# A selective scan on one core: TensorE's scan-stage work put into two row groups of 64

## The chip, the core and the metric

The kernel runs on one core of a Trainium2 chip. A core has TensorE (matrix multiplies and transposes, into PSUM), VectorE, ScalarE, GpSimd (called POOL in the profile) and SyncE (SP, which here issues nearly all DMAs). They run side by side and wait for each other through semaphores. The metric is the device time of one execution in microseconds, as the median of several runs. All data are fp32.

## The reference

Two residual blocks work on x of shape (8, 56, 56, 192). Block 0 is a gated Toeplitz mixer (group norm, three projections, Toeplitz products along both image axes, an output projection). Block 1 is a visual state-space block, and nearly all of the time goes there:

```python
xz = gn(x) @ W_in.T                     # 192 -> 2 x 384;  xc, z = split
xc = silu(depthwise_conv3x3(xc))        # (8, 384, 56, 56)
xs = [four snake orders of the image, and the four reversed]    # K = 8 directions, L = 3136
dts, B, C = split(einsum(xs, x_proj_weight), [12, 16, 16])      # per direction
delta = softplus(einsum(dts, dt_projs_weight) + bias)           # (8, K, 384, L)
h[l] = exp(delta[l] * A) * h[l-1] + (delta[l] * xs[l]) * B[l]   # 16 states a channel
y[l] = sum over states of h[l] * C[l];  y += D * xs             # summed over directions
out = x + (layernorm(y) * silu(z)) @ W_out.T
```

## The kernel before

For each of the 8 images the kernel runs three stages one after the other: a preparation (input projection, 3x3 convolution, the three stored snake orders written to DRAM as xo), the **scan stage**, and a last stage that reads the directions' outputs back, sums them and does the layer norm, the gate and the output projection. Block 0 runs ahead of all this. The change touches the scan stage alone, and the weights that the host lays out for it.

**Chunks, groups, pairs, units.** A direction's 3136 positions are cut into chunks of W = 127. Four chunks make a group (508 positions); a direction has six such groups and a last one of a single chunk. The 384 channels are NB = 3 blocks of 128, d = 0, 1, 2. A pair is two chunks of one block, and it has four units: chunk c = 0, 1, each with states 0 to 7 (half 0) and 8 to 15 (half 1). So a full group is 24 units, a direction 150, an image 1200, the kernel 9600. One unit is:

- `products` (L733), TensorE: the scan's additive term bx, 8 states x 127 positions, from dut (the transposed delta*x, positions on partitions) and bd (the B values laid on a diagonal). It is made in two turns; in each, positions 0 to 63 and 64 to 126 are two row groups of TensorE that write to different banks, and the banks are swapped in the second turn. A ScalarE instruction (`between`) stands between the turns.
- `exps` (L688), ScalarE: da = exp(delta*A), four instructions a unit on average, a pair of das ahead at most. `before` (L756), ScalarE: copies the carried state into column 0 of bx. `keep` (L774), ScalarE: takes the carry out after a pair.
- `scan` (L761), VectorE: one scan instruction over 8 x 128 elements.
- `times_c` (L779), POOL: hc = h * C.
- `sums` (L789), TensorE: eight transposes of hc[:, n] (128 channels x 127 positions), accumulated in PSUM, so they sum over the states: yps, positions on partitions. It takes four tiles of 127 x 128 (pair parity, chunk) in one bank.
- `summed` (L699), ScalarE: yps to yt after a pair, and a store to DRAM after three.

**What a group needs ahead of its units.** Weights (once per direction) and xs are loaded (`load`). `project` (L540), TensorE: px, the 12 + 16 + 16 projected rows, padded to XR = 64, one matmul of 508 columns for each d, accumulated. `projected` (L553), ScalarE: pxs = px + a bias row of 1. `to_dram` and `broadcast` (SP) send the C rows through DRAM to all partitions (cbt); `diagonal_out` (L631) and `diagonal_in` (L637) do the like for B with bd. `steps` (L575), TensorE: pd = dt_w x pxs, 13 rows, for each d; `stepped` (L584), ScalarE, copies it to delta; `softplus` (L588), ScalarE, once for all three blocks, with a load of another activation table on either side of it. `product` (L612), POOL: du = delta * xs for a chunk, 128 x 381. `turn` (L617), TensorE: three transposes of du into pt; `turned` (L621), ScalarE: copies pt to dut. px, pd and pt share one PSUM buffer in a bank of its own (pool pmisc, one buffer). A last group of one chunk has `all_steps` (L595) and `all_stepped` (L604), one step for all three blocks.

**What sets the order.** The kernel writes each engine's order out by hand, step by step: in step t the loop issues the second bx turn of unit t + 1, the first of t + 2, `keep` of t - 1, `summed` of t - 4, `sums` of t - 3, planned ScalarE work, up to two exponentials, `before` of t + 1, the `between` instruction, planned VectorE work, the scan of t, planned TensorE work, `times_c` of t - 1, planned POOL and SP work, more exponentials as a credit allows, and "late" work (softplus). `plan` says at which step, counted from the first unit f of the group, planned work comes. bx has three buffers, h and hc four each. Engines are kept apart by PSUM tensor and bank: an access waits for the earlier ones of other engines in the program's order that touch the same bank of the same tensor.

## Time and profile before

| | us |
|---|---|
| Median of 3 runs (32,992.14 to 33,007.02) | 32,998.84 |
| The profiled execution's own time | 33,035.09 |
| Its span, first to last instruction | 33,033.3 |
| Its eight scan stages together | 25,014.3 |
| All the rest | 8,019.0 |

The mean granted TensorE clock is 0.968 over the span and 1.00 in the scan stages. A row of the profile names the line, the engine, the operation, what is written from what, partitions x elements, and how often; then busy time and mean duration in ns, or start and length in us. "PEld" is TensorE's weight load, which runs beside its matmuls. The part after "<-" in brackets is how long the engine was idle before and what ended that; "issue" means that nothing seen in the profile did. A matmul in fp32 appears as two instructions, a transpose as one.

### The profile page before, as it was taken

Reading aid. Unit: us, or ns where it says so; the run is one execution under the profiler, and the core shown is the slowest. Engines: PE = TensorE matmul, PEld = TensorE weight load, DVE = VectorE, ACT = ScalarE, POOL = GpSimd, SP = SyncE. Lnnn points to the kernel's source line nnn. Section 1 sums busy time; section 2 is a strip of 40 time slices with the busy share of each in tenths; the row PEclk is TensorE's granted clock in tenths of the full one; section 3 lists DMA queues with packets and bytes.
Section 4 is the critical chain, followed back from the end, with each engine's and each line's share of the span. In section 5 each row is a group of like instructions: output and inputs, shape, how many; then the busy total and the mean of one; then the engine's idle time right before and its main releaser. Section 6 shows DMA issues by size and latency. Waiting matters only on the chain. (4 is left out here: it accounts for less than half of the span.)

```text
span 33033.3 us, 535851 instructions
## 1 busy us (share of the span) xinstructions
PE 30106.0 (91%) x195376; PEld 20579.6 (62%) x195376; DVE 23832.6 (72%) x13236; ACT 23299.1 (71%) x63562; POOL 22361.9 (68%) x11632
## 2 busy tenths in 40 slices
PE   8999899979998899979998899979998899979998
PEld 5555566646665566646665566646665566646665
DVE  3444588848886588848886688848886688848886
ACT  2332588838886588838886688838885688838885
POOL 0000588838886588838886588838885688838885
PEclk9999999989999999989999999989999999989999
DMA  3222344444444444444444344444444344444444
GB/s 78 60 60 56 116 126 127 127 127 125 126 129 132 120 127 128 126 126 128 125 126 138 119 125 126 129 128 124 127 128 133 118 129 125 126 127 130 125 126 132
DMA packets 4719499, 3974.35 MB, mean 120 GB/s; under 512 B 3678496, under 2 KB 4401888, under 8 KB 4611008
## 3 DMA queue, kind: packets, MB, share of 16 engines
q1 hardware_dynamic: 4558272, 3778.58, 40.3%
q10 hardware_dynamic: 158592, 161.47, 1.9%
q8 instruction: 1552, 25.43, 0.3%
q14 instruction: 1083, 8.87, 0.1%
HBM read 3406.62 MB, written 547.17 MB: 120 GB/s over the span
## 5 line engine op out<-in xcount | busy, mean ns | idle before, releaser
L761 DVE TENSOR_TENSOR_SCAN h<-da,bx 128x1024 f32<-128x1024 f32 x9600 | 21447.9, 2275 | 3899.2 <-ACT bx L756 2956.6
L779 POOL TENSOR_TENSOR hc<-h,cbt 128x1016 f32<-128x1016 f32 x9600 | 20694.4, 2177 | 2470.8 <-DVE h L761 1973.9
L688 ACT ACTIVATE da<-delta,A_logs 128x254 f32<-128x254 f32 x39936 | 17115.8, 490 | 856.1 <-PE bx L733 807.1
L733 PE MATMUL bx<-bd,dut 63*128 63x252 f32 (+1 forms) x76800 | 11032.5, 404 | 1071.2 <-ACT bx L756 376.8
L789 PEld LDWEIGHTS yps<-ident,hc 128*127 128x127 f32 x76800 | 9246.5, 190 | 3384.3 <-issue 2081.0
L789 PE MATMUL yps<-ident,hc 128*127 128x128 f32 x76800 | 11065.2, 287 | 196.4 <-ACT bx L756 142.7
L733 PEld LDWEIGHTS bx<-bd,dut 63*128 63x128 f32 (+1 forms) x76800 | 6506.3, 187 | 4540.3 <-ACT da L688 878.0
L422 POOL MEMSET xp<- 128x58 f32 x96 | 10.3, 194 | 5692.5 <-DMA x<-x1d 3395.9
L612 POOL TENSOR_TENSOR du<-delta,xs 128x381 f32<-128x381 f32 x1600 | 1605.7, 1004 | 712.7 <-ACT bx L756 477.3
L1004 ACT ACTIVATE sq<-yc 128x1344 f32<-128x1344 f32 x56 | 74.0, 1322 | 2111.9 <-DMA yk<-yt 1781.2
L540 PE MATMUL px<-xs,xpw 128*64 128x508 f32 (+1 forms) x2688 | 1304.4, 576 | 226.7 <-DMA xs<-xo 198.4
L575 PE MATMUL pd<-pxs,dtw 13*128 13x508 f32 x2304 | 1296.6, 642 | 17.9 <-ACT delta L584 10.7
L584 ACT COPY delta<-pd 128x508 f32<-128x508 f32 x1152 | 669.7, 581 | 727.2 <-PE pd L575 721.4
L756 ACT COPY bx<-h 128x8 f32<-128x8 f32 x4608 | 753.2, 163 | 594.1 <-PE bx L733 324.2
L446 PE MATMUL pc<-xp,dg 128*128 128x448 f32 x3024 | 1138.0, 538 | 0.0
L774 ACT COPY carry<-h 128x8 f32<-128x8 f32 x4608 | 884.1, 192 | 320.9 <-DVE h L761 302.6
L756 ACT COPY bx<-carry 128x8 f32<-128x8 f32 x4992 | 820.4, 164 | 400.3 <-PE bx L733 369.1
L468 POOL COPY xo<-xc 128x672 f32<-128x672 f32 x112 | 80.6, 749 | 1392.8 <-issue 754.8
L699 ACT COPY yt<-yps 127x256 f32<-127x256 f32 (+1 forms) x2496 | 890.2, 357 | 175.6 <-PE yps L789 122.3
L446 PEld LDWEIGHTS pc<-xp,dg 128*128 128x128 f32 x3024 | 571.2, 189 | 565.5 <-issue 565.5
L470 DVE COPY xo<-xc 128x672 f32<-128x672 f32 x112 | 90.3, 848 | 1129.3 <-ACT xc L453 1129.3
L406 DVE TENSOR_SCALAR x1n<-x,gstat 96x448 f32<-96x448 f32 x224 | 103.6, 505 | 1078.8 <-DMA x<-x1d 803.5
(121 smaller groups left out, 17121.0 us busy)
## 6 DMA issues: line engine op xcount, KB each, us to landing
cbt<-cd SPq DMA_DIRECT2D x768, 2032.0 KB
bd<-bd SPq DMA_DIRECT2D x1600, 512.0 KB
xs<-xo SPq DMA_DIRECT2D x384, 762.0 KB
yt<-yt SPq DMA_DIRECT2D x1536, 190.5 KB
yk<-yt ACTq DMA_DIRECT2D x1792, 84.0 KB
yk<-yt SPq DMA_DIRECT2D x1792, 84.0 KB
xo<-xo SPq DMA_DIRECT2D x168, 672.0 KB
xc<-xc SPq DMA_DIRECT2D x112, 672.0 KB
```

The costliest lines, as they stand in the source:

```text
L446: nc.tensor.matmul(pc, dg[:, d, j, :], xp[d][:, t * RT + dy : t * RT + dy + RT, dx : dx + HW], start=(j == 0), stop=(j == 8),)
L540: nc.tensor.matmul(self.px[:, : self.n], weights[self.k][0][:, d], self.xs[:, d], start=(d == 0), stop=(d == NB - 1),)
L575: nc.tensor.matmul(self.pd[:, : self.n], weights[self.k][1][:, d * 128 : (d + 1) * 128], self.pxs[0 : R + 1], start=True, stop=True,)
L612: nc.gpsimd.tensor_mul(self.du, self.delta[:, :, part], xs[:, :, part])
L688: yield nc.scalar.activation(da[:, : G.ncs, n, 1:], src.rearrange("p (c t) -> p c t", t=W), AF.Exp, scale=an[:, G.k, self.d, col : col + 1],)
L699: nc.scalar.copy(G.yt[:, : G.ncs, self.d * 128 : (self.d + 1) * 128], yps[:, self.i % 2, : G.ncs])
L733: mm = nc.tensor.matmul(self.bx[:, 4 * q : 4 * q + 4, 1 + 64 * r : 1 + 64 * r + nr], dut[rows, P.d * 128 : (P.d + 1) * 128], bd[rows, n0 : ...
L756: return nc.scalar.copy(self.bx[:, :, 0], prev)
L761: nc.vector.tensor_tensor_scan(self.h.rearrange("p n t -> p (n t)"), das[2 * (P.i % 2) + self.half][:, self.c].rearrange("p n t -> p (n t) ...
L774: nc.scalar.copy(P.carry[:, P.d, states(self.half)], self.h[:, :, W])
L779: nc.gpsimd.tensor_tensor(self.hc, self.h[:, :, 1:], G.cb[P.s][:, states(self.half), self.c * W : (self.c + 1) * W], ALU.mult,)
L789: nc.tensor.matmul(yps[:, self.P.i % 2, self.c], lhsT=self.hc[:, n], rhs=ident, start=(self.half == 0 and self.c == 0 and n == 0), stop=(s ...
```

## The change

- The two PSUM pools of one bank become one tensor `acc` of two banks, [128, 2, 512]. Its first half-banks hold yps, its second half-banks a scratch `mis` for px, pd and the turns. Index r of the bank is the row group (partitions 0 to 63 and 64 to 127 of the operands).
- `sums`: each transpose becomes two, of the channels of each row group, with a moving operand of 64 columns instead of 128; 16 loads and 16 matmuls a unit instead of 8 and 8.
- `project`: the contraction over 128 channels is split in two row groups that write partial sums to two banks, in two calls e of 254 positions each; XR grows to 128, so that the 12 step rows stand at partitions 0 and again at 64. `projected` copies bank 0 with the bias, and the new `added`, VectorE, adds bank 1.
- `steps`: the first 254 positions by row group 0, the last 254 by row group 1, with the weights given twice and padded with zeros to 64 rows. `stepped` copies both banks in one instruction. `all_steps` and `all_stepped` split in the like way.
- `turn`: three transposes become six halves. `turned` copies both banks in one instruction.
- `product`: odd chunks go to VectorE, even ones stay on POOL.
- The plan: TensorE's planned work comes at even steps and the read of it by ScalarE one step later. `projected` at f - 23 and f - 21 (one at f - 19 before), `stepped` at f - 19, - 17, - 15 (f - 17, - 15, - 13), softplus at f - 13 (f - 12), `to_dram` and the first `diagonal_out` at f - 20 (f - 19), loads at f - 36 (f - 34). The turns stay at f - 10, - 8, - 6, - 4.
- In the loop, planned ScalarE work is issued ahead of `sums` instead of after it, and planned VectorE work after the scan instead of ahead of it.

The diff, cut to its core:

```diff
-            pmisc = st.enter_context(tc.tile_pool(name="pmisc", bufs=1, space=PSUM))
-            pyp = st.enter_context(tc.tile_pool(name="pyp", bufs=1, space=PSUM))
+            pacc = st.enter_context(tc.tile_pool(name="pacc", bufs=1, space=PSUM))
...
-            yps = pyp.tile([W, 2, 2, 128], F32, name="yps")
+            acc = pacc.tile([128, 2, 512], F32, name="acc")
+            yps = acc[:, :, :256].rearrange("p r (i c x) -> p r i c x", i=2, c=2)
+            mis = acc[:, :, 256:]
+            def rows(r):
+                return slice(64 * r, 64 * r + 64)
...
+                def project(self, e):
+                    h = self.half
+                    e = self.n // h - 1 - e if self.rev else e
+                    for d in range(NB):
+                        for r in range(2):
+                            nc.tensor.matmul(
+                                mis[:, r, :h],
+                                weights[self.k][0][rows(r), d],
+                                self.xs[rows(r), d, e * h : e * h + h],
+                                start=(d == 0),
+                                stop=(d == NB - 1),
+                            )
...
+                    self.part = self.pxs[:, e * h : e * h + h]
+                    self.src = src[:, 1]
+                    nc.scalar.activation(self.part, src[:, 0], AF.Identity, bias=pxb)
+                def added(self):
+                    nc.vector.tensor_add(self.part, self.part, self.src)
...
-                    nc.tensor.matmul(
-                        self.pd[:, : self.n],
-                        weights[self.k][1][:, d * 128 : (d + 1) * 128],
-                        self.pxs[0 : R + 1],
...
+                    for r in range(2):
+                        nc.tensor.matmul(
+                            mis[:, r, :h],
+                            weights[self.k][1][rows(r), d * 128 : (d + 1) * 128],
+                            self.pxs[rows(r), r * h : r * h + h],
...
-                    nc.gpsimd.tensor_mul(self.du, self.delta[:, :, part], xs[:, :, part])
+                    eng = nc.vector if c % 2 else nc.gpsimd
+                    eng.tensor_mul(self.du, self.delta[:, :, part], xs[:, :, part])
...
-                        nc.tensor.transpose(self.pt[:, d * 128 : (d + 1) * 128], self.du[:, d], ident)
+                        for r in range(2):
+                            nc.tensor.transpose(
+                                mis[:W, r, 64 * d : 64 * d + 64], self.du[rows(r), d], ident[rows(r), rows(r)]
+                            )
...
                     for n in range(HN):
-                        nc.tensor.matmul(
-                            yps[:, self.P.i % 2, self.c],
-                            lhsT=self.hc[:, n],
-                            rhs=ident,
-                            start=(self.half == 0 and self.c == 0 and n == 0),
...
+                        for r in range(2):
+                            nc.tensor.matmul(
+                                yps[:W, r, self.P.i % 2, self.c],
+                                lhsT=self.hc[rows(r), n],
+                                rhs=ident[rows(r), rows(r)],
+                                start=(self.half == 0 and n == 0),
...
+                credit -= 0.5 * do("ACT", t)
                 if (U := unit(t - 3)) is not None:
                     U.sums()
-                credit -= 0.5 * do("ACT", t)
...
-                do("DVE", t)
                 if (U := unit(t)) is not None:
                     U.scan()
+                do("DVE", t)
                 do("PE", t)
```

## The prediction

> **What bounds the kernel now.** I read the busy times first, then the eight scan stages one by one, then one group of 24 units in order of time. (A difference of 0.2% is about what a measurement of this kernel can tell from none.)

> The page's busy times, over the whole span:

> ```profile
> PE 30106.0 (91%) x195376; PEld 20579.6 (62%) x195376; DVE 23832.6 (72%) x13236; ACT 23299.1 (71%) x63562; POOL 22361.9 (68%) x11632
> ```

> The same by stretches: first the sum over the eight scan stages, then one regular group of the fourth (busy us of each engine, then clock and DMA):

> ```profile
> sum 25014.30, PE 23821.09 PEld 16885.12 DVE 21447.60 ACT 21667.94 POOL 22127.35; mean PE 2977.64 PEld 2110.64 DVE 2680.95 ACT 2708.49 POOL 2765.92
> ```

> ```profile
> 15799.87:15861.12 61.25, 59.31 (x410) 42.22 (x409) 53.63 (x24) 53.57 (x150) 55.44 (x30) 1.00 0.44 125
> ```

> So 25,014 us of the 33,033 are scan. There a group takes 61.25 us and TensorE is busy for 59.31 of it, against 53.6 for VectorE and ScalarE: TensorE bounds. What does it spend it on? Its timeline in that group (start, length, engine, line):

> ```profile
> 15801.32 1.15 PE L789 MATMUL yps<-ident,hc 128*127 128x128 f32 x8
> 15802.40 1.13 PE L733 MATMUL bx<-bd,dut 64*128 64x256 f32 x8
> 15803.45 1.15 PE L789 MATMUL yps<-ident,hc 128*127 128x128 f32 x8
> ...
> 15806.67 1.07 PE L540 MATMUL px<-xs,xpw 128*64 128x508 f32 x2
> 15807.67 1.13 PE L733 MATMUL bx<-bd,dut 64*128 64x256 f32 x8
> ```

> A unit costs 1.08 (sums) + 1.05 (bx) = 2.14 us from start to start; px adds 1.00. Now the weight loads of another stretch:

> ```profile
> 8509.46 0.73 PEld L733 LDWEIGHTS bx<-bd,dut 64*128 64x128 f32 x8
> 8510.52 0.96 PEld L789 LDWEIGHTS yps<-ident,hc 128*127 128x127 f32 x8 [0.33 <-issue]
> ```

> Before the sums (128 rows) the weight path stands 0.33 us waiting for nothing but issue, in unit after unit, because bx ran in row groups of 64. Net work is less: eight loads take 0.96 and three (L617) 0.41, so 0.11 per transpose, 0.88 for eight; bx x8 takes 1.13 and the x4 of a lone turn 0.70, so 0.43 for two passes in both row groups, 0.86 for four. 0.88 + 0.86 = 1.74: 0.40 us of 2.14 is changing the array's shape.

> [...]two half loads must overlap. [...]the loads of bx show it, two of 0.18 us within 0.19 us, four within 0.30:

> ```profile
> 8509.46 0.19 PEld L733 LDWEIGHTS bx<-bd,dut 64*128 64x128 f32 x2
> ...
> 8509.46 0.30 PEld L733 LDWEIGHTS bx<-bd,dut 64*128 64x128 f32 x4
> ```

> [...]In the group above the sums already waited 0.7 us for the yt copy of their bank.

> **The change, part by part, for a group of 24 units.**
> - *Sums*: 16 loads and 16 matmuls of 64 moving columns for 8 and 8 of 128. In parallel row groups the pair costs one load, 0.11: still 0.88 a unit. That 64-row transposes run is seen at L263 (eight of 64 columns in 0.63 us, 0.056 each), and that TensorE takes an instruction every 26 ns at L276 (22 loads in 1.22 us, a matmul to each); four per 0.11 us are needed. No drain on either side: 24 x 0.40 = 9.6 us gone.
> - *px*: three steps of 1.00 become two bursts of 3 x 2 passes x 254 columns in both groups: 0.215 us per pass (bx, 256 columns), 1.28 each, 2.56 in all for 3.0.
> - *pd*: 3 x 1.05 (15818.22 to 19.26) becomes 3 x 2 x 0.213 = 1.28. *Turns*: 12 loads of 0.11, 1.32.
> - TensorE's sum: 24 x 1.74 + 2.56 + 1.28 + 1.32 = 46.9, where the same sum of before is 24 x 2.14 + 3.0 + 3.15 + 1.4 = 58.9. It stops being the bound; the next is VectorE.
> - *VectorE*: back-to-back scans start 2.19 us apart (x2 in 4.46, each 2.27), 52.6 for 24. New: two `added` of 254 columns from PSUM, by L1002 (448 columns 616 ns, 1.05 ns a column from L1024 and L1028) 0.41 each; two du of 381 columns, by L1024 0.55 each. 1.9 us, all on the path: the scan behind them waits. 54.5.
> - *POOL* loses two du of 1.00: 24 x 2.17 + 2.0 = 54, not quite the bound. *ScalarE* has two pxs copies of 254 columns (0.47 by the 679 ns for 508 and 362 for 127) for one of 0.68, +0.26 on 53.6 that overlap at their ends.
> - *New waits*: yps and the scratch share two banks, so in the nine steps with a read of the scratch (2 pxs, 3 delta, 4 dut) the sums stand behind ScalarE's copy, which stands behind carry (end of a scan) and yt: by carry 0.2, yt 0.37, copy 0.58 it ends about 1.1 us after the scan, while TensorE wants the bank at 0.6 (it waits for the same scan to free a bx buffer, then makes half a bx, 0.43). 9 x 0.5 = 4.5 us of TensorE at most, behind which bx wait; TensorE has 54.5 - 46.9 = 7.6 to spare, and bx are made a unit ahead. I take nothing, at most 0.2 each on the path (1.8). After a pxs, both `added` and the next sums wait for each other's bank; 0.1 each.
> - *DMAs*: weights grow from 13 to 128 rows and 64 to 128 columns, once per direction and 24 units ahead; to_dram goes a step earlier and now waits for `added` on SP, with the diagonal writes queued behind it; the reads that need them come over ten steps later. Nothing, with steps of 2.3 us as the cover; without it bd would come late.
> - *What is late next*: the two stalls that ScalarE makes. A pd step today:

> ```profile
> 15818.22 1.11 PE L575 MATMUL pd<-pxs,dtw 13*128 13x508 f32 x2
> ...
> 15819.42 0.58 ACT L584 COPY delta<-pd 128x508 f32<-128x508 f32 x1 [0.73 <-PE pd L575]
> ...
> 15820.71 0.17 ACT L756 COPY bx<-carry 128x8 f32<-128x8 f32 x1
> ...
> 15820.98 2.29 DVE L761 TENSOR_TENSOR_SCAN h<-da,bx 128x1024 f32<-128x1024 f32 x1 [0.83 <-ACT bx L756]
> ```

>   The 0.73 us wait for a late pd makes the scan 0.83 late. With pd done 0.6 + 0.88 + 0.43 = 1.9 us after the step began, before ScalarE asks in the next, this goes (three pd, and 0.85 + 1.52 at the px). The second stays:

> ```profile
> 15834.55 1.28 ACT L588 ACT_TABLE_LOAD   x1
> 15835.84 1.47 ACT L588 ACTIVATE delta<-delta 128x1524 f32<-128x1524 f32 x1
> 15837.22 0.16 ACT L756 COPY bx<-h 128x8 f32<-128x8 f32 x1
> ...
> 15837.48 4.57 DVE L761 TENSOR_TENSOR_SCAN h<-da,bx 128x1024 f32<-128x1024 f32 x2 [1.45 <-ACT bx L756]
> ```

>   Softplus holds ScalarE for 2.75 us and the scan for 1.45. It moves a step, and I keep 1.5. Steps with carry, yt, copy, two exponentials and the bx copy hold about 1.95 us of ScalarE in 2.19; I add 0.8 for these and for the bank turns.

> The sum: 52.6 + 1.9 + 1.5 + 0.8 = **56.8 us** a group, 4.45 or 7.3% less. I give every scan stage that share: 0.0727 x 25,014 = 1,817. The other 8,019 us are not touched. 33,035 (the profiled execution's own time, 2 us over its span) - 1,817 = 31,218; the median of the runs lies 36 lower: **31,180**.

> **Rivals.**
> - *The half loads of the transposes do not overlap.* No row of before shows transposes in two row groups at once. Bound from below: 0.11 a pair. From above: 0.22, a unit of 16 x 0.11 + 0.86 = 2.62, a group of 24 x 2.62 + 5.2 = 68.1 + 1.9 of idle as now = 70: +14.3%, 36,600 us, **slower**. It decides from 0.17 a pair ((61.25 - 1.9 - 5.2) / 24 = 2.26, less 0.86, by 8). Against it: the bx loads. I take 0.11. Chance 0.08.
> - *Bank turns tie TensorE to ScalarE.* If each of the nine delays the scan by 0.5, 4.5 us go and the gain with them: 33,000. Against: the unit of lead. At 0.3 each 2.7 are lost, 32,300. Chance 0.12 for both together, of which 0.06 within or above 0.2% of before.
> - *VectorE becomes nearly the whole bound*, softplus hidden by a ScalarE that TensorE no longer holds up (its waits for bx, pd and px are 1.6 + 1.1 + 2.2 + 0.8 = 5.7 us a group): 54.5 + 0.5 = 55.0, -10.2%, 30,450. Chance 0.15.
> - *It does not do what it says*: a drain stays between sums and bx, say 0.2 of the 0.4. TensorE 46.9 + 4.8 = 51.7, still under 54.5; bx come later, about 58.5: 31,900. Inside the likeliest case's range.

> **Numbers.** The likeliest case, 0.65, has 30,600 to 31,950 for its own range. To it come the larger gain, and half of the bank turns: 30,450 to 32,500 holds about 0.83; left out are the serial loads and turns that eat everything. Faster by over 0.2%: 0.65 + 0.15 + 0.06 = 0.86; within: 0.05; slower: 0.09.

> **What would show it.** In the profile after, sums of x16 in about 0.9 to 1.0 us, no 0.33 idle before them, TensorE near 47 to 50 us in a group of 57, scans 2.19 apart in most steps, no scan late at a delta copy, one late by 1 to 1.5 at softplus, and VectorE's busy share in the scan near 95%. Sums of 1.7 us or TensorE still at 97% would prove the sum wrong; so would scans late after every turn, with TensorE waiting for dut, delta or pxs.

## The result, and the profile after

The changed kernel takes 38,623 us (38,534 to 38,680) where the kernel before, beside it on the chip, took 33,002: a ratio of 1.1701 [1.1679, 1.1724]. The forecast was 31,180 us and faster: it is **wrong in sign**.

The page of the kernel after, busy times and granted clock over the span (40 slices, in tenths of full speed; before, nearly every digit was 9):

```profile
PE 34813.8 (90%) x286960; PEld 30031.1 (78%) x286960; DVE 24584.5 (64%) x14836; ACT 23597.0 (61%) x64010; POOL 21923.7 (57%) x10864
...
PEclk9998777676777677677767767677767676776776
```

TensorE was to be busy for less time, and is busy 4,708 us more. The busy times of the eight scan stages, summed, and then of one regular group (busy us of PE, PEld, DVE, ACT and POOL; last the clock, the DMA share and GB/s):

```profile
sum 30605.90, PE 28506.27 PEld 26280.30 DVE 22183.77 ACT 21961.62 POOL 21703.39; mean PE 3563.28 PEld 3285.04 DVE 2772.97 ACT 2745.20 POOL 2712.92
```

```profile
18074.62:18149.89 75.27, 72.57 (x639) 68.31 (x638) 55.45 (x29) 54.36 (x150) 54.33 (x28) 0.68 0.39 113
```

The scan stages grew by 5,592 us (25,014 to 30,606), the span by 5,585: all of it lies there. A regular group takes 75 us for 61, and TensorE's clock in it is 0.68 for 1.00. So the first question is not what TensorE does but how fast its clock runs. The same group again, cut where its clock changes (columns as above):

```profile
18084.30:18107.70 23.40, 22.58 (x276) 19.36 (x274) 22.23 (x12) 20.61 (x62) 18.98 (x9) 1.00 0.12 20
18107.70:18111.60 3.90, 2.02 (x28) 1.76 (x26) 2.60 (x2) 3.85 (x8) 3.89 (x4) 0.94 0.74 78
18111.60:18145.00 33.40, 33.40 (x242) 32.62 (x244) 23.30 (x12) 22.18 (x61) 22.79 (x12) 0.50 0.66 207
```

In the first stretch the clock is full and VectorE is busy for 22.2 of 23.4 us: this is the kernel that was forecast. In the second TensorE is busy for only 2.0 of 3.9 us. In the third it runs at half clock, and is busy for **all** of 33.4 us: slowed by two, it bounds the group. The trace's clock record has the fall at 18111.14 and the return 47.8 us later.

The timeline of the first stretch (start, length, engine, line), a run of scans with one pd step and two units in it:

```profile
18090.60 19.70 DVE L796 TENSOR_TENSOR_SCAN h<-da,bx 128x1024 f32<-128x1024 f32 x9
...
18101.37 0.65 PE L594 MATMUL acc<-pxs,dtw 64*128 64x254 f32 x4
...
18102.07 0.58 ACT L603 COPY delta<-acc 128x508 f32<-128x508 f32 x1
...
18104.76 1.07 PEld L825 LDWEIGHTS acc<-ident,hc 64*127 64x127 f32 x16
...
18104.97 1.00 PE L825 MATMUL acc<-ident,hc 64*127 64x64 f32 x16
...
18105.80 1.08 PE L768 MATMUL bx<-bd,dut 63*128 63x252 f32 x8
...
18106.71 1.01 PE L825 MATMUL acc<-ident,hc 64*127 64x64 f32 x16
```

Sixteen half transposes take 1.00 us, nothing idles before their weight loads in this unit, a unit is 1.74 us from sums to sums (18104.97 to 18106.71), the copy of delta waits for nothing, and nine scans run without a gap. Then softplus, at the second stretch:

```profile
18108.58 1.28 ACT L609 ACT_TABLE_LOAD   x1
18108.78 1.00 PE L825 MATMUL acc<-ident,hc 64*127 64x64 f32 x16
...
18109.87 1.47 ACT L609 ACTIVATE delta<-delta 128x1524 f32<-128x1524 f32 x1
...
18111.56 2.07 PE L768 MATMUL bx<-bd,dut 64*128 64x256 f32 x8 [1.78 <-ACT bx L791]
18111.60 4.56 DVE L796 TENSOR_TENSOR_SCAN h<-da,bx 128x1024 f32<-128x1024 f32 x2 [1.30 <-ACT bx L791]
...
18113.40 1.82 PE L825 MATMUL acc<-ident,hc 64*127 64x64 f32 x16
```

The scan is 1.30 us late, where 1.5 was forecast. But TensorE, which is ahead now, stands 1.78 us idle (1.04 at this place before), and from the fall at 18111.14 on the same bx x8 takes 2.07 us for 1.08 and the same sums 1.82 for 1.00. A unit then costs TensorE about 3.4 us (scans at 18074.62 and 18077.98, both in the half-clock stretch before this one) against VectorE's 2.19.

### The profile page after: what moved, and what is told of

Read it like the earlier page. It is cut to its first block, busy times and chain, and to the rows that moved or that the text cites. A ratio compares the mean times of both kernels' runs of the same rounds, so it can differ in the third digit from the quotient of the medians.

```text
span 38618.7 us, 724883 instructions
## 1 busy us (share of the span) xinstructions
PE 34813.8 (90%) x286960; PEld 30031.1 (78%) x286960; DVE 24584.5 (64%) x14836; ACT 23597.0 (61%) x64010; POOL 21923.7 (57%) x10864
## 5 line engine op out<-in xcount | busy, mean ns | idle before, releaser
L768 PE MATMUL bx<-bd,dut 64*128 64x256 f32 (+1 forms) x76800 | 15567.8, 521 | 1742.0 <-ACT bx L791 516.9
L825 PEld LDWEIGHTS acc<-ident,hc 64*127 64x127 f32 x153600 | 14920.2, 256 | 1422.3 <-issue 769.9
L825 PE MATMUL acc<-ident,hc 64*127 64x64 f32 x153600 | 14072.4, 333 | 425.7 <-ACT delta L603 130.3
L768 PEld LDWEIGHTS bx<-bd,dut 64*128 64x128 f32 (+1 forms) x76800 | 10366.8, 258 | 2949.9 <-ACT da L722 922.0
L422 POOL MEMSET xp<- 128x58 f32 x96 | 10.2, 190 | 5674.3 <-DMA x<-x1d 3404.6
L551 PE MATMUL acc<-xs,xpw 64*128 64x254 f32 x9984 | 1853.6, 505 | 247.0 <-DMA xs<-xo 208.4
L551 PEld LDWEIGHTS acc<-xs,xpw 64*128 64x128 f32 x9984 | 1450.0, 265 | 299.1 <-issue 243.4
L734 ACT COPY yt<-acc 127x256 f32<-127x256 f32 (+1 forms) x2496 | 900.2, 361 | 1144.5 <-PE acc L643 426.3
L643 PE MATMUL acc<-ident,du 64*127 64x64 f32 x9600 | 1371.3, 391 | 53.7 <-POOL du L638 39.3
L643 PEld LDWEIGHTS acc<-ident,du 64*127 64x127 f32 x9600 | 1233.6, 307 | 63.7 <-POOL du L638 45.0
L649 ACT COPY dut<-acc 127x384 f32<-127x384 f32 x1600 | 763.5, 477 | 541.0 <-PE acc L643 541.0
```

Of the source, the lines that this page charges most:

```text
L551: nc.tensor.matmul(mis[:, r, :h], weights[self.k][0][rows(r), d], self.xs[rows(r), d, e * h : e * h + h], start=(d == 0), stop=(d == NB - 1),)
L643: nc.tensor.transpose(mis[:W, r, 64 * d : 64 * d + 64], self.du[rows(r), d], ident[rows(r), rows(r)])
L649: nc.scalar.copy(dut.rearrange("w (d r x) -> w r d x", d=NB, r=2), mis[:W, :, : 64 * NB].rearrange("w r (d x) -> w r d x", d=NB),)
L734: nc.scalar.copy(out.rearrange("w c (r x) -> w r c x", r=2), yps[:W, :, self.i % 2, : G.ncs])
L768: mm = nc.tensor.matmul(self.bx[:, 4 * q : 4 * q + 4, 1 + 64 * r : 1 + 64 * r + nr], dut[at, P.d * 128 : (P.d + 1) * 128], bd[at, n0 : n0 ...
L825: nc.tensor.matmul(yps[:W, r, self.P.i % 2, self.c], lhsT=self.hc[rows(r), n], rhs=ident[rows(r), rows(r)], start=(self.half == 0 and n == 0),
```

## The experiments

**Theory.** Two factors: a *fall* where ScalarE holds TensorE for some half of a window, and a *length*, set by what runs at half clock: the half-row sums do not bring the clock back, the dense px burst does. (In the trace of the kernel after, 495 phases of half clock begin in a scan stage; px ran in the last window of 3.41 us of 426 of them, and in 364 of the 4,848 windows in which the clock stayed low.) **Rivals**: the bank turns or late data are the loss and the low clock only follows from the idle time; or the clock is low because TensorE has slack, whatever its instructions are. Below, "falls" are the phases of half clock in each trace's clock record that lie in a scan stage (in every run eight of them, one a stage, had begun just before it), and "half-clock time" is their time there; the table after the last run has them all.

**1. Filler bursts.** Three bursts a group of six matmuls like px, into the scratch, read by nobody.

```diff
+            for G in groups:
+                for step in (-14, -12, -2):
+                    if G.nch > 1 and ("PE", G.first + step) not in plan:
+                        at("PE", G.first + step, G.warm)
```

> The changed kernel with three bursts of TensorE work added to each full group, at the even steps f - 14, f - 12 and f - 2 that have none: six matmuls of 254 columns (twelve passes, 1.28 us at full clock) into the scratch, which nobody reads; nothing else differs. Clock theory (TensorE's granted clock falls to one half at the softplus stall and the light mix of bx and half transposes cannot lift it again): the bursts keep it up or lift it within a few steps, mean clock in the scan stage over 0.9 where it is 0.70 now, a group 57 to 60 us for 75, 31,000 to 32,500 us in all. Rival (the turns on the shared banks, or the number of instructions, cost the time and the low clock only follows from the waiting): 3 x 1.28 us more work for TensorE in a group, 38,600 to 41,000 us, the clock still near 0.7.

Measured: 36,208 us, 1.0960 [1.0943, 1.0976], clock 0.87. Added work, 2,400 us less time: against the rival, but short of the range of the theory, which had the bursts keep the clock up as well. A phase of half clock lasts 15.6 us for 35.9; the falls stay (478 for 503).

**2. Exp for Softplus**, to be rid of the table loads around it (1.28 us each in the kernel before); log(1 + x) is left out.

```diff
-                    nc.scalar.activation(v, v, AF.Softplus)
+                    nc.scalar.activation(v, v, AF.Exp)
```

> The changed kernel with Exp in the place of both Softplus activations (the logarithm of 1 + x is left out), so that ScalarE loads no other table around them: the stall of 2.75 us becomes 1.5. Clock theory: TensorE is not idle long enough in regular groups for the clock to fall there, so the mean clock of the scan stage rises from 0.70 to 0.85 or more (low phases are left where directions begin), 32,000 to 34,500 us. Rival (bank turns): the 2 x 1.28 us of table loads saved in a group are all there is to win, at most 64 x 6.2 x 2.6 = 1,000 us, 37,600 us or more, clock as now.

Measured: 35,860 us, 1.0858 [1.0842, 1.0874]. Slower than the theory's range and far faster than the rival's: the stall sets off much of the loss, but not all. 440 falls are left, at other waits.

**3. The sums in 128 rows again**, eight transposes into one bank; all else of the change stays.

```diff
-                        for r in range(2):
-                            nc.tensor.matmul(
-                                yps[:W, r, self.P.i % 2, self.c],
-                                lhsT=self.hc[rows(r), n],
-                                rhs=ident[rows(r), rows(r)],
+                        nc.tensor.matmul(
+                            yps[:W, self.c],
+                            lhsT=self.hc[:, n],
+                            rhs=ident,
```

> The changed kernel with its sums put back to full transposes of 128 rows and 128 moving columns, into one half of bank 0 (no second buffer for the other pair; the wait for yt is there already). px, pd, turns, du, bank turns and the order stay as changed. Clock theory, in the form that the half-width moving operand of the sums is what makes the mix too light: the clock comes back within a window of 3.4 us after each stall, as in the kernel before, mean over 0.95; the drains of 0.4 us a unit return, a group 59 to 62 us, 32,000 to 33,500 us in all. Rival (bank turns or the plan): they are untouched and bank 0 is shared as before, so the time stays at 37,000 to 39,500 us.

Measured: 35,046 us, 1.0608 [1.0592, 1.0624]. This is the cleanest split of the two factors: **483 falls for 503, but 5.3 us long for 35.9**. The time lies between the two ranges, since another price remains. Regular groups take 65.6 us at nearly full clock, and the largest waits of TensorE in the fourth scan stage and around it (us in total, times, longest) say why:

```profile
PE bx L766 <- DMA bd<-bd: 101.1, 31, 8.3
```

In one group after the other bx waits for bd. Over the fourth stage alone the wait is 112.5 us in 37 times; in the kernel before it was 2.5 us in five.

**4. Half the sums in the kernel before.** Only the first 64 channels are transposed (and yps zeroed once); the sums of the other 64 are left out. Nothing else of the change.

```diff
-                            yps[:, self.P.i % 2, self.c],
-                            lhsT=self.hc[:, n],
-                            rhs=ident,
+                            yps[:, self.P.i % 2, self.c, :64],
+                            lhsT=self.hc[:64, n],
+                            rhs=ident[:64, :64],
```

> The kernel before with one edit: each transpose of the sums takes the first 64 of its 128 channels only (the other half of the sums is left out), eight loads of 64 rows and eight matmuls of 64 moving columns a unit. No bank turns, no second bank, no new waits, no work more on any engine; TensorE needs 1.74 us a unit at full clock for 2.14, since bx and sums now have one array shape. Clock theory: with the light mix the clock stays at one half after each stall, a unit then takes about 3.4 us, and doing half of the sums makes the kernel slower than before: 34,500 to 39,000 us, mean clock of the scan stage 0.6 to 0.8. Rival (bank turns, order, instruction count): none of these is here, so it gets faster, 30,500 to 32,000 us, clock as before.

Measured: 43,564 us, 1.3182 [1.3160, 1.3204], with *less* work. Two regular groups:

```profile
20116.58:20202.62 86.04, 85.37 (x409) 70.75 (x409) 54.53 (x24) 54.94 (x149) 55.71 (x29) 0.60 0.33 92
20202.62:20288.15 85.53, 85.13 (x409) 70.50 (x409) 54.55 (x25) 55.02 (x149) 55.86 (x30) 0.60 0.33 96
```

TensorE has no slack here (85.1 of 85.5 us) and still the clock is 0.60; a phase lasts 75 us, and the time is above the theory's range. Bank turns, px, pd and the order are those of before. So neither rival makes the low clock; the shape of the sums does.

The run also shows that a fall needs no stall, against the first factor of the theory. One of its falls, at 20051.33, comes after this window:

```profile
20047.92:20051.33 3.41, 3.23 (x22) 2.21 (x20) 3.29 (x2) 2.31 (x8) 1.52 (x2) 1.00 0.32 36
```

TensorE was busy for 3.23 of 3.41 us, with bx, half sums and a pd of 13 rows. Of the 393 phases that begin in its scan stages, 253 come after a window with TensorE busy for over 90%, each with a pd in it; in the kernel after, none of 495 does.

**5. bd early**: the read of chunk 1 (and of a lone chunk) at f - 9, ahead of the yt stores in SP's queue.

```diff
-                        at("SP", start + 2 * c + 1, self.diagonal_in, c)
+                        at("SP", f - 9 if c < 2 else start + 2 * c + 1, self.diagonal_in, c)
```

> The changed kernel with one DMA moved: the read of the diagonal B image (bd) of the second chunk goes out at step f - 9 beside that of the first (f - 7 before), and that of a one-chunk group at f - 9 too, so that on SP and in its DMA queue it stands ahead of the two yt stores of step f - 8 and not behind them. DMA theory: in a regular group bx of unit 2 waits 4 to 5 us for this bd, since it lands after both stores; that stall at the group's head (3.4 + 7.4 us between scans where 2.2 + 2.2 is the least) shrinks to what the low clock makes of it, and so 2 to 5 us of 75 go in each of the 320 groups: 37,000 to 38,000 us, clock still about 0.70. Rival (the head is slow from the clock alone, and bd is late only because everything is): under 300 us, 38,300 or more.

Measured: 36,814 us, 1.1151 [1.1134, 1.1168], a little more than was expected of it. The bd wait (50.4 us in 12 times between 16842 and 20651 us in the kernel after) is not among the seven largest of TensorE in that stretch of run 5, which go down to 22.5, and 1,809 us go: a second cause, and one that also cost clock (409 falls for 503).

**6. bd early and bursts at every free even step** from f - 22 on (the edit of run 5, and that of run 1 at more steps).

> The changed kernel with that DMA moved and with the bursts of TensorE work of run e1_warm at every even step from f - 22 on that has none, so around the one-chunk groups and direction changes too. If low clock and late bd are the two causes and nothing else is: a regular group 56.5 to 58.5 us (step sum of the prediction 56.8, 65 in e1_warm), the groups at direction changes 65 to 75 for 76 to 83, 32,000 to 33,800 us in all, mean clock of the scan stage 0.93 or more. If a third cause (bank turns) is behind the rest: a regular group stays over 61 and the time over 34,500.

Measured: 33,854 us, 1.0258 [1.0241, 1.0275], just above the first range; the first groups of the directions take 82.6 us, not 65 to 75. A regular group, now at full clock:

```profile
16013.53:16073.32 59.79, 55.77 (x676) 47.82 (x676) 55.59 (x29) 53.16 (x151) 54.47 (x27) 1.00 0.47 136
```

Here the forecast's own sum can be audited: 59.8 for 56.8, and VectorE's rows over three such groups name the gap (busy us, mean ns, idle before):

```profile
L650 DVE TENSOR_TENSOR du<-delta,xs 128x381 f32<-128x381 f32 x6 | 6.4, 1060 | 0.0
L583 DVE TENSOR_TENSOR pxs<-pxs,acc 128x254 f32<-128x254 f32 x6 | 2.5, 420 | 5.2 <-ACT da L734 5.2
```

The 1,060 ns of a du are a mean of two kinds. Here are both of the first of these groups, with what POOL has under way, and then the row of the two in the kernel after's group above:

```profile
16051.85 4.62 POOL L826 TENSOR_TENSOR hc<-h,cbt 128x1016 f32<-128x1016 f32 x2
16053.80 0.63 DVE L650 TENSOR_TENSOR du<-delta,xs 128x381 f32<-128x381 f32 x1
...
16062.04 4.62 POOL L826 TENSOR_TENSOR hc<-h,cbt 128x1016 f32<-128x1016 f32 x2
16063.14 1.49 DVE L650 TENSOR_TENSOR du<-delta,xs 128x381 f32<-128x381 f32 x1
```

```profile
L638 DVE TENSOR_TENSOR du<-delta,xs 128x381 f32<-128x381 f32 x2 | 1.1, 532 | 0.0
```

In run 6's regular groups the first du takes 0.63 us and the second 1.49 (medians of 192), and both end 0.41 us after the hc that POOL was in when they started. In the kernel after POOL is in no hc as most of them start (322 of 384), and both medians are 0.53.

**7. bd early and 128-row sums** (5 and 3 together).

> Run e3_full_rows (full transposes in the sums) with that DMA moved as in e5_bd_early, no bursts. DMA theory: the head of a regular group (2.2 + 9.5 us between scans there) comes down to about 4.5, a group from 65.5 to 58 to 60 us, and the small groups gain as much: 32,000 to 33,300 us, about the time before. Rival (the head is slow for another reason): 34,500 to 35,100 us.

Measured: 33,439 us, 1.0133 [1.0118, 1.0148], near the theory's range and far from the rival's. Regular groups take 60.1 us, but the first group of a direction 75.1, against 67.4 before.

**8, 9, 10. Softplus as Ln(Exp(x) + 1)**, Exp in place of the copy of delta: with half-row sums and bd early (8), with 128-row sums and bd early (9), and in the kernel before with bd early (10). That no table load would stand between Exp and Ln was my assumption; no trace had shown it.

```diff
-                    nc.scalar.copy(
+                    nc.scalar.activation(
...
+                    nc.scalar.activation(self.delta[:, d], self.delta[:, d], AF.Ln, bias=unity)
...
-                        at("late", f - 13, self.softplus)
```

> The changed kernel with the early bd read (as in the run that had it alone, 36,814 us) and softplus written as Ln(Exp(x) + 1): Exp takes the place of the copy of delta out of PSUM and Ln follows in place[...]. It still computes the whole function. Clock theory: the clock falls where ScalarE holds TensorE for over half a window, and softplus is the one such place in a regular group; without it the clock stays at or above 0.95 in the scan stages, a regular group takes 57 to 59 us, the first group of a direction 68 to 76, and the time is 31,800 to 32,700 us, under the kernel before. Rival: the half-width work cannot hold the clock by itself, whatever ScalarE does, and any small stall drops it: the clock stays under 0.90, groups at 63 us or more, the time at 34,000 us or more.

> The same with the sums as 128-row transposes again (33,439 us with softplus as it was). Clock theory: this kernel lost 1,765 us to low-clock phases of a window or two each, mostly one a group at softplus; they go, the clock is at 0.97 or more, regular groups take 58 to 59.5 us and the time is 32,400 to 33,000 us. If the half-row sums are faster per unit as forecast (1.74 instead of 2.14 us of TensorE) this one stays slower than the run with half-row sums by 300 us or more. Rival: with the stall gone the two are level, because VectorE bounds both, within 150 us of each other.

> The kernel before with the same two edits (early bd read, softplus as Ln(Exp(x) + 1)), for what they are worth without the change. Theory: TensorE bounds it at 59.3 us of busy time a group, so the softplus stall of 1.45 us is what they can take away: regular groups 60 to 60.8 us for 61.3, the first group of a direction 64 to 66 for 67.4, the time 32,400 to 32,800 us. Rival: TensorE uses the stall to catch up and the stall is free: 32,950 to 33,050 us.

Measured: 44,352 us, 1.3442 [1.3422, 1.3462]; 37,391 us, 1.1332 [1.1313, 1.1351]; 37,455 us, 1.1349 [1.1332, 1.1366]. The stalls that were to go did not, so none of the three was the test that it was meant to be, and for one reason. ScalarE's table loads in the first of them (times, busy us, mean ns):

```profile
L726 ACT ACT_TABLE_LOAD x1200 | 1539.6, 1283 | 12.8
L608 ACT ACT_TABLE_LOAD x1152 | 1478.0, 1283 | 21.0
```

The kernel after has 448 and 384 at these two places. Every Ln of a full group got a load ahead of it (1,152 for 1,152) and the next exponential another, 1.283 us each. (The expectation of run 9 starts from 1,765 us lost in run 7; run 7's trace has 1,275 us at half clock in the scan stages.) The runs became another experiment: three stalls a group, not one. With 128-row sums the clock then falls 1,027 and 867 times, for 4.5 and 6.6 us each; with half-row sums 847 times, for **33.7** us. The same stalls, a fall five to seven and a half times as long.

**11. A version with little left of the change**: run 7 with px by 128-row matmuls into one bank, the one that these sums leave free (no `added`), all du on POOL, softplus back at f - 12. pd, the turns, the two px steps and the order stay.

```diff
-                        at("late", f - 13, self.softplus)
+                        at("late", f - 12, self.softplus)
...
-                        at("DVE" if c % 2 else "POOL", start + 2 * c - 1, self.product, c)
+                        at("POOL", start + 2 * c - 1, self.product, c)
```

> The run with 128-row sums and the early bd read (33,439 us), with three more parts of the change undone: px by 128-row matmuls into one bank (so no added on VectorE), all du on POOL, softplus back at f - 12. What stays of the change: pd and turns in two row groups with banks of their own, two px steps of 254 positions, planned ScalarE work ahead of the sums. Theory: the stalls of 1.7 and 1.3 us in the second and fourth step of a regular group are the two added and their waits, those of 0.6 and 1.2 us later are du, and the 7.06 us in the middle of a direction's first group is softplus between two blocks of exponentials; they go, a regular group takes 58 to 59.5 us for 60.0, the first group 66 to 70 for 75.1, and the time is 32,300 to 32,950 us, under the kernel before. Rival: these stalls are TensorE's own (px and turns beside sums), whoever does the rest: groups stay at 60, and the time at 33,200 to 33,450 us.

Measured: 32,982 us, 0.9983 [0.9976, 0.9989]: just above the range expected, far below the kernel after, and 0.17% under the kernel before, which is no more than a tie in practice. A regular group:

```profile
15705.20:15764.57 59.37, 57.40 (x434) 43.91 (x433) 53.45 (x25) 53.10 (x151) 55.37 (x29) 1.00 0.44 133
```

The 59.4 us, and 70.3 for a direction's first group, lie within or at the edge of the theory's figures. Of the single stalls (what the interval between two scans has over 2.19 us), the two at du halved (1.8 to 0.9 us together, from run 7), that of the group's second step fell from 1.7 to 0.9, and that of the fourth stayed (1.3 and 1.4): that one fits the rival (px stands in TensorE's order whoever does the rest).

**12. Run 6 with softplus at f - 12.**

> The run with filler bursts and the early bd read (33,854 us) with softplus one step later, at f - 12 as in the kernel before; nothing else. Theory: at a direction's start softplus of f - 13 falls between two blocks of eight exponentials that must be done, which is the 7.06 us wait; the first group falls from 82.6 to 77 to 80 us, the other groups stay within 0.5 us, and the time is 33,500 to 33,750 us. Rival: the wait is the two blocks alone: 33,800 to 33,900 us.

Measured: 33,972 us, 1.0283 [1.0269, 1.0297]. The interval of 7.06 us between two scans in a direction's first group became 3.22 (and the one after it 2.96 for 2.21), and that group fell from 82.6 to 80.1 us, nearly as expected. The time did not fall; it is above both ranges. Half-clock time rose (3,879 us for 3,286), which may be why, but that was not tested.

All runs side by side (scan stages; us; the last two columns are the mean time of a direction's first group and of its third to fifth):

| Kernel | Sums | Falls | Half-clock time | Mean of one | First group | Regular |
|---|---|---|---|---|---|---|
| before | 128 rows | 36 | 190 | 5.3 | 67.4 | 61.3 |
| after | 64 | 503 | 18,065 | 35.9 | 81.4 | 75.1 |
| 1 bursts | 64 | 478 | 7,442 | 15.6 | 82.9 | 65.1 |
| 2 Exp | 64 | 440 | 8,554 | 19.4 | 78.9 | 65.5 |
| 3 | 128 | 483 | 2,558 | 5.3 | 74.1 | 65.6 |
| 4 before, half sums | 64 | 401 | 30,076 | 75.0 | 90.5 | 88.1 |
| 5 bd early | 64 | 409 | 12,895 | 31.5 | 75.9 | 73.2 |
| 6 bursts, bd | 64 | 289 | 3,286 | 11.4 | 82.6 | 59.9 |
| 7 bd | 128 | 196 | 1,275 | 6.5 | 75.1 | 60.1 |
| 8 Ln, bd | 64 | 847 | 28,564 | 33.7 | 84.8 | 92.3 |
| 9 Ln, bd | 128 | 1,027 | 4,668 | 4.5 | 71.7 | 73.4 |
| 10 before, Ln, bd | 128 | 867 | 5,742 | 6.6 | 76.4 | 73.3 |
| 11 | 128 | 140 | 829 | 5.9 | 70.3 | 59.4 |
| 12 bursts, bd | 64 | 238 | 3,879 | 16.3 | 80.1 | 60.1 |

The column "mean of one" sorts the kernels by the rows of their sums alone: 4.5 to 6.6 us with 128 rows, 19 to 75 with 64, and 11 to 16 with 64 and bursts.

## Why the prediction was wrong, point by point

- **The drain, half loads, px and pd: right.** At full clock the unit is 1.74 us of TensorE as summed (1.75 in run 4, where bx and sums also run in 64 rows; 2.14 before), 16 sums 1.00. One load of 64 rows takes 187 ns on average, where one of 128 rows took 190, but 16 of them take 1.07 us, where 8 took 0.96, so they do overlap. Of the rest, pd 0.49 a step to the next matmul for 0.43, with no wait behind it (the late scans at delta are gone), px 1.34 a burst for 1.28. The rivals on serial half loads and on bank turns did not come about (the longest wait of the sums for the copy of a full group's delta out of their banks was 0.6 us in the fourth scan stage).
- **The step that failed: TensorE's sum, "It stops being the bound; the next is VectorE".** In a regular group TensorE is busy for 72.6 of 75.3 us, not 46.9 of 56.8, and is the bound. The term that is missing is the granted clock, 0.68 there. Every TensorE duration in the sum was read at a clock of 1.00, and "TensorE 46.9" of 56.8 us left it idle for 10 us a group where it had been 2. That clock was taken as a constant of the stage; it changes with what TensorE is given (in a regular group 1.00 before, 0.68 after, 0.60 in run 4, 1.00 in run 6). No case in the range had it, so all of them lay on the wrong side. The runs put its price, in a regular group, at 73.2 - 59.9 = 13.3 us (run 5 against run 6, both with bd early; run 6 carries its bursts' work).
- **"Net work is less": in time, not in what keeps the clock up.** Sums of 64 moving columns in two row groups do in 1.00 us what took 1.15, and there the clock is 0.68 for 1.00; half the sums in one row group (run 4) do not hold it either (0.60).
- **"DMAs: nothing": wrong.** The step named a cover, steps of 2.3 us and over ten steps, and even what would go: "without it bd would come late". It came late at a group's head. What I had counted were the diagonal writes; the read of chunk 1 behind the yt stores was left out. It stood behind them before too, but SP's queue runs later now: in regular groups its issue starts 12.2 us ahead of the group's first scan in run 3, and 15.9 us in the kernel before (medians of 192). At nearly full clock it is worth 65.6 - 60.1 = 5.5 us a group (runs 3 and 7), a part of which is clock, since the wait makes it fall too (483 falls and 196).
- **VectorE's 1.9 us: mis-sized.** The work was read rightly (a du 0.53 for 0.55 in the kernel after, `added` 0.42 for 0.41); the waits were not. From run 6's rows, at the forecast's pace, a du takes 1.06 us, since it ends only after POOL's hc, and `added` has 5.2 / 6 = 0.87 of waiting each, where 0.1 was allowed. So 2 x 1.06 + 2 x 1.29 = 4.7 us for 1.9 + 0.2. With 52.6 for the scans and 1.6 for softplus (an interval of 3.76 for 2.19 in run 7; forecast 1.5) this gives an estimate of 58.9: even at a full clock, with bd on time, the gain of a group would have been some 4%, not 7.3%. Run 6, with its bursts, measures 59.8.
- **"I give every scan stage that share": wrong.** A direction's first group loses most in every version (67.4 us before, 75 to 83 in runs 5 to 7). Softplus a step earlier is part of it: the interval there went from 3.65 to 7.06 us, and run 12 took 2.5 us of the group back. The rest was not tested.

Left open is what the granted clock goes by. Sums of 128 rows and columns keep it (1.00 in a regular group of the kernel before, with 27.6 of TensorE's 59.3 busy us in them), those of 64 do not (0.68 in the kernel after). The records' busy time is not the measure (run 4).

One measure fits the traces, as an estimate. Count each matmul by its columns, at 0.84 ns each (a pass of 256 takes 0.215 us; twice that at half clock, where bx x8 took 2.07 us for 1.08), and by the share of the 128 rows that it uses. Over the scan stages of all fourteen traces, 6,115 of 6,191 falls come after a window of 3.41 us that is filled to 0.42 or less, and only 1,210 of the 69,756 windows that kept the full clock are. Of the windows that ended a phase of half clock, 5,207 of 6,191 are filled to 0.75 or more, against 2,752 of the 30,030 in which it went on. A unit of 128-row sums fills (0.86 + 0.86) / 2.14 = 0.80 of its time, one of 64-row sums in two row groups (0.86 + 0.43) / 1.74 = 0.74, and one of run 4 (0.86 + 0.22) / 1.74 = 0.62. This would be why only the first brings the clock back. But it was found in the traces afterwards and no run tested it: rows and columns were halved together in every run, and a sum of 64 rows by 128 columns was not tried.

## What to carry to other kernels

Read the granted clock as an output, not as a constant: where an edit takes TensorE off the bound, or turns its work into smaller pieces, ask what a stall of a microsecond or two will do to the clock (here it fell after 3.41 us with TensorE busy for 1.96), and whether the work that follows brings it back (phases of half clock lasted 5.3 us with the 128-row sums of run 3, and 35.9 with the 64-row sums of the kernel after). The cheap test is to cut such a piece of work in half in the old kernel: if it gets slower at a lower clock, the clock decides (run 4: 32% slower, at 0.60 for 1.00). And when a group gets faster, list every transfer by its slack, not only those the edit moves.

## What was not expected of the hardware

- TensorE was busy by the records for 33.40 of 33.40 us, at a clock of 0.50 throughout (kernel after), and its clock fell after windows in which it was busy for over 90% (253 of 393 falls of run 4): it can be the bound and not be granted its clock.
- Halving the sums of a kernel bound by TensorE made it 32% slower (run 4), and adding matmuls that nobody reads made one 6% faster (run 1 against after).
- VectorE's product of 128 x 381 took 0.53 us where POOL was in no hc (the kernel after); where POOL was, it ended 0.41 us after that hc, and so took 0.63 or 1.49 (run 6). POOL needs 1.00 for the same product (the kernel before).
- Exp and Ln in turn cost a table load of 1.283 us each way, 2,352 loads in run 8.
